# A graph layer on one core: another PSUM ring for one product, and a second engine for half of the copies in front of the router

## The chip, the core and the metric

The kernel runs on one core of a Trainium2 chip. The metric is the device time of one execution in microseconds. The profile comes from one further execution, and its times count from the start of its span. In the profile PE is TensorE (PEld its weight loads), DVE is VectorE, ACT is ScalarE, POOL is GpSimd and SP is SyncE, which issues most DMAs.

## What is computed

There are 1250 nodes of 1024 features and 40000 edges, sorted by target. A two-layer graph network is added to the input, and a mixture of experts is added to that:

```python
h   = relu(x_n @ W_self0 + mean0 @ W_neigh0 + b0)     # x_n = layernorm(x); mean over the sources of a node
out = h @ W_self1 + mean1 @ W_neigh1 + b1
x   = x + out
t   = layernorm(x)
logits = silu(t @ rw1 + rb1) @ rw2 + rb2              # router, top 2 of 8 experts
y   = t + sum_e w[t, e] * (silu(t @ ew1[e] + eb1[e]) @ ew2[e] + eb2[e])
out = x + y
```

All data is float32 in the reference.

## The kernel before, in words

The nodes are cut into ten blocks of up to 128 rows; the last one (block 9, `b9`) has 98. The work runs in stages, one after the other on PE: the counts of edges and the first layer (to 434 us), the second layer, the router (from about 778 us), and a loop over 23 tiles of tokens sorted by expert (from about 919 us).

**The second layer.** Its products by `W_neigh1` and `W_self1` go half by half of the columns, through `y_half` (twice) and `own_half` (twice, `h` = 0 and 1). Each of these four makes five pairs of blocks with `two_blocks` (lines 630 to 686): pairs 0 to 3 take the blocks j and 4+j, and the fifth pair takes the blocks 8 and 9. A pair is a Strassen-like scheme: seven products of four matmul steps each (line 648), in PSUM tiles `pa`, `pb` from the pool `mm` (tile name `ps`), and `pc`, `pd` from the pool `mmb` (tile name `psb`). Both pools have three buffers of one bank. In pairs 0 to 3 the product by `A22` is added to `pc` (line 679). In the fifth pair, where block 9 is shorter than 128 rows, it goes to a tile of its own, `pe` (line 682), taken from `mmb`, and `store` adds `u3` to it on DVE.

**What follows on each block.** In the last of the four halves, `own_half(w_last, ws_last, 1, finish)`, `finish(b)` runs for both blocks of a pair when its products are done (line 793). It calls `after_layers` (line 330): the layernorm (two `bn_stats` of 512 columns, lines 316 and 318, the aggregate, line 319, a square root on ACT, line 320, the reciprocal, line 322, and the 1024-wide normalisation on DVE, line 323), a store of the result to `t_d`, a POOL addition of the normalised row to `xa` (line 337), and a store of `xa` to the output (line 338). `finish` then hands the block to a queue of at most two, so that `turn_back` (line 805) works on the block that was finished two calls earlier. After the fifth pair `turn_back` empties the queue.

**`turn_back`.** A block is transposed on PE in two groups of four 128-column squares (line 814). A group is one tile of the pool `tpp` (`tp`, two buffers), of 4 x 128 float32 in each partition, which is one PSUM bank. Four copies of one square each bring it to `hT1`, where the router reads it; before the change ACT makes all four:

```python
for i in range(4):
    nc.scalar.copy(hT1[:, q + i, blk(b)], ps[:, i, :m])
```

**The router.** `moe` opens its own pools in the banks that `mm` and `mmb` leave. `route_two` is the same scheme as `two_blocks`, with 512-column operands: its sums of tokens (`token_sums`, T1, T2, T4) and T3 are written by DVE (line 140). T1, T2, T4 lie in `xw`, which takes the memory of `xa` and `more`, so T1 has to wait until the last block's store of `xa` has landed. `route(w0, 0, LAST)` (line 1167) is work on the last 226 tokens that PE does while T1 and T2 are made.

**What sets the order.** In these stages no order is written by hand. A planner walks the program in its order and puts the instructions on the engines' queues by its own model of their durations; at run time each engine takes its queue strictly in that order. It also sets the waits that the use of tiles needs. Orders written out by hand (`manual_schedule`) are in the opening and in the loop over tiles.

Of the kernel before, what the change touches and what calls it, by code (L numbers as in the profile page):

```python
# [10 lines left out]
F32 = mybir.dt.float32  # L11
# [10 lines left out]
P = 128  # L22
# [7 lines left out]
def kernel(  # L30
# [21 lines left out]
    nc = tc.nc  # L52
# [6 lines left out]
    QW = D // 4  # L59
# [14 lines left out]
    def blk(b):  # L74
        return slice(b * P, b * P + rows[b])
# [16 lines left out]
    hT1 = L[:, :NT].rearrange("p (k n) -> p k n", k=KD)  # L92
# [46 lines left out]
    def tt(o, a, b_, op):  # L139
        nc.vector.tensor_tensor(o, a, b_, op)  # L140
# [200 lines left out]
    def gnn_windows():  # L341
# [4 lines left out]
        mm = st.enter_context(tc.tile_pool(name="mm", bufs=3, space=PSUM))  # L346
# [177 lines left out]
        for q in range(4):  # L524
# [8 lines left out]
            if q == 0:  # L533
# [4 lines left out]
                for c0, n in cchunks:  # L538
                    ps = mm.tile([P, 512], F32, name="ps")
# [7 lines left out]
            for c0, n in cchunks:  # L547
                for d in (2 * q, 2 * q + 1):
                    ps = mm.tile([P, 512], F32, name="ps")
# [12 lines left out]
            if q == 0:  # L562

                dinv_p = small.tile([P, NB], F32, name="dinv_p")
                for b in range(NB):
                    m = rows[b]
# [7 lines left out]
        mmb = st.enter_context(tc.tile_pool(name="mmb", bufs=3, space=PSUM))  # L574
# [59 lines left out]
        def two_blocks(ws, j, u, store, amid=False):  # L634


            A11, A12, A22, S1, S2, S3, S4 = ws
            if j < NA:
                b, b2 = j, NA + j
                t1, t2, t3, t4 = (t[:, :, j * P : (j + 1) * P] for t in (T1, T2, T3, T4))  # L640
            else:
                b, b2 = b8, b9
                t1, t2, t3, t4 = Te1, Te2, Te3, Te4
            m2 = rows[b2]

            def product(ps, rows_of, w, first):
                for k in range(KB):
                    nc.tensor.matmul(  # L648
                        ps, rows_of(k), w[:, k, :], start=(first and k == 0),
                        stop=(k == KB - 1), skip_group_check=not first,  # L650
                    )

            u2, u3 = u[:, 0, :], u[:, 1, :]
            pa = mm.tile([P, 512], F32, name="ps")[:, :QW]
            product(pa, lambda k: hT1[:, k, blk(b)], A11, True)
            nc.scalar.copy(u2, pa)
            yield
            if amid:
                product(pa, lambda k: hT1[:, KB + k, blk(b)], A12, False)
                store(b, 0, pa, None)  # L660
                yield
            pb = mm.tile([P, 512], F32, name="ps")[:, :QW]
            product(pb, lambda k: t2[:, k, :], S2, True)
            tt(u2, u2, pb, ALU.add)
            if not amid:
                product(pa, lambda k: hT1[:, KB + k, blk(b)], A12, False)
                store(b, 0, pa, None)
            pc = mmb.tile([P, 512], F32, name="psb")[:, :QW]
            product(pc[:m2], lambda k: t3[:, k, :], S3, True)
            if m2 < P:  # L670

                past = slice(m2 // LQ * LQ, P)
                nc.scalar.copy(u3[past], u2[past])
            tt(u3[:m2], u2[:m2], pc[:m2], ALU.add)
            pd = mmb.tile([P, 512], F32, name="psb")[:m2, :QW]
            product(pd, lambda k: t1[:, k, :], S1, True)
            store(b2, 1, pd, u3[:m2])
            if m2 == P:
                product(pc, lambda k: t4[:, k, :], A22, False)
                store(b, 1, pc, u2)  # L680
            else:
                pe = mmb.tile([P, 512], F32, name="psb")[:, :QW]
                product(pe, lambda k: t4[:, k, :], A22, True)
                store(b, 1, pe, u3)
            product(pd, lambda k: hT1[:, KB + k, blk(b2)], S4, False)
            store(b2, 0, pd, u2[:m2])
# [16 lines left out]
        with tc.tile_pool(name="y1", bufs=1, side="right") as y1:  # L703
# [3 lines left out]
            def y_half(ws, h):  # L707
                def store(b, c, ps, u):
                    m = rows[b]
                    if u is not None:  # L710
                        t = spare()[:m]
                        tt(t, u, ps, ALU.add)
                        ps = t
                    cs = slice(c * QW, (c + 1) * QW)
                    split(yh[:m, b, cs], yl[:m, b, cs], ps)

                def pair(j, amid=False):
                    return two_blocks(
                        ws, j, us[:, 2 * (j % 2) : 2 * (j % 2) + 2, :], store, amid
                    )  # L720

                if h == 0:

                    two = [pair(j, True) for j in range(2)]
                    for _ in range(2):
                        for p in two:
                            next(p)
                    for p in two:
                        list(p)
                for j in range(0 if h else 2, NA + 1):  # L730
                    list(pair(j))
# [44 lines left out]
        def own_half(w, ws, h, done):  # L776
            def store(b, c, ps, u):
                m = rows[b]
                v = xa[:m, b, h * HALF + c * QW : h * HALF + (c + 1) * QW]
                if u is None:  # L780
                    tt(v, v, ps, ALU.add)
                else:
                    t = spare()[:m]
                    tt(t, u, ps, ALU.add)
                    nc.gpsimd.tensor_tensor(v, v, t, ALU.add)

            for j in range(NA + 1):
                list(two_blocks(ws, j, us[:, 2 * (j % 2) : 2 * (j % 2) + 2, :], store))
                if h == 0 and j == 1:
                    ws_last.extend(weight_sums(w_last, more[:, 2 * WQ : -2048]))  # L790
                for b in (j, NA + j) if j < NA else (b8, b9):
                    done(b)
# [3 lines left out]
        def finish(b):  # L796

            t = row_of((0, 1, 3)[n_done[0] % 3])
            n_done[0] += 1
            after_layers(b, xa, t)  # L800
            turned.append((b, t))
            if len(turned) > 2:
                turn_back()
# [3 lines left out]
        def turn_back():  # L807

            b, t = turned.pop(0)
            m = rows[b]  # L810
            for q in range(0, KD, 4):
                ps = tpp.tile([P, 4, P], F32, name="tp")
                for i in range(4):
                    nc.tensor.transpose(
                        ps[:, i, :m], t[:m, (q + i) * P : (q + i + 1) * P], ident[:m, :m]
                    )
                for i in range(4):
                    nc.scalar.copy(hT1[:, q + i, blk(b)], ps[:, i, :m])

        ws_last = []  # L820
        own_half(w_half, ws, 0, lambda b: None)
# [4 lines left out]
        while turned:  # L826
            turn_back()
# [920 lines left out]
```

## Time and profile before

| | us |
|---|---|
| median of 3 runs | 1121.33 |
| lowest, highest run | 1120.26, 1122.6 |
| the profiled execution | 1122.76 |
| its span in the profile | 1120.8 |
| PE busy | 1084.8 |
| DVE busy | 473.7 |
| ACT busy | 189.2 |
| POOL busy | 335.9 |

The profiled execution took 1122.76 us, 1.96 us more than its span, and 1.4 us more than the median. The copies of `turn_back` are 80 of 128 or 98 columns on ACT, between 735.1 and 785.1 us; the 72 wide ones had a mean of 285 ns. When several of them follow each other they overlap: 12 of them took 2.27 us from the start of the first to the end of the last.

In a line of the timeline the columns are the start in us, the duration in us, the engine, the line, the operation with output and input, and how many there are; in brackets stands the idle time before it and what ended it. In a line of the waits stand the waiting engine and the thing waited for, then the total in us, the number of times, and the longest. In the chain, each piece is the start, the length and the work.

### The profile page before, as it was taken

Reading aid. Unit: us, or ns where it says so; the run is one execution under the profiler, and the core shown is the slowest. Engines: PE = TensorE matmul, PEld = TensorE weight load, DVE = VectorE, ACT = ScalarE, POOL = GpSimd, SP = SyncE. Lnnn points to the kernel's source line nnn. Section 1 sums busy time; section 2 is a strip of 40 time slices with the busy share of each in tenths; the row PEclk is TensorE's granted clock in tenths of the full one; section 3 lists DMA queues with packets and bytes.
Section 4 is the critical chain, followed back from the end, with each engine's and each line's share of the span. In section 5 each row is a group of like instructions: output and inputs, shape, how many; then the busy total and the mean of one; then the engine's idle time right before and its main releaser. Section 6 shows DMA issues by size and latency. Waiting matters only on the chain.

```text
span 1120.8 us, 13458 instructions
## 1 busy us (share of the span) xinstructions
PE 1084.8 (97%) x4825; PEld 803.8 (72%) x4825; DVE 473.7 (42%) x1171; ACT 189.2 (17%) x431; POOL 335.9 (30%) x447
## 2 busy tenths in 40 slices
PE   6999999999999999999999999999999999999993
PEld 5555556888888888888888878887544487676762
DVE  8777787763121236332234132355522173222221
ACT  4301001001111111110011000023111134232321
POOL 2899999900000000013002202254000013332321
PEclk9999999999999999999999999999999999999997
DMA  7011011010100020033003280343970456767762
GB/s 241 30 38 39 2 38 39 1 38 1 38 1 1 1 75 20 1 113 120 27 1 142 101 275 1 94 174 152 321 228 1 150 188 169 193 178 193 194 170 47
DMA packets 62318, 107.34 MB, mean 96 GB/s; under 512 B 8906, under 2 KB 35690, under 8 KB 62240
## 3 DMA queue, kind: packets, MB, share of 16 engines
q1 hardware_dynamic: 51392, 79.69, 20.8%
q0 software_dynamic: 7056, 23.88, 9.1%
q10 hardware_dynamic: 3792, 2.79, 0.8%
q8 instruction: 42, 0.69, 0.3%
q14 instruction: 36, 0.29, 0.1%
HBM read 80.74 MB, written 27.42 MB: 96 GB/s over the span
## 4 chain that ended last, share of the span: by engine, by line
PE 75%; DMA 14%; DVE 4%; issue 4%; POOL 1%; ACT 1%; SPq 0%; POOLq 0%; DVEq 0%; ACTq 0%
PE ps L516 12%; DMA out_dram<-L 12%; PE ps L453 12%; PE psb L648 11%; PE ps L744 8%; PE ps L648 8%; PE ps L552 8%; PE ps L1214 4%; PE ps L1228 3%; PE cnt L414 3%; PE ps L1167 1%; DMA more<-in_L_gnn_W_self_dram 1%; DVE xw L140 1%; DVE L L140 1%; PE tp L306 1%
## 5 line engine op out<-in xcount | busy, mean ns | idle before, releaser
L404 POOL TENSOR_SCALAR ol<-lane,keys 125x128 f16<-125x128 f16 x320 | 193.8, 624 | 23.3 <-DVE oh L411 23.3
L453 PE MATMUL ps<-h0T,L 128*128 128x498 f32 (+2 forms) x384 | 148.0, 518 | 0.2 <-ACT h0T L309 0.2
L740 POOL TENSOR_TENSOR L<-L 128x512 f32<-128x512 f32 (+1 forms) x20 | 27.7, 1394 | 383.4 <-DMA L<-in_x_dram 383.4
L516 PE MATMUL ps<-L,h0T 128*128 128x256 f32 (+1 forms) x640 | 142.0, 379 | 0.0
L516 PEld LDWEIGHTS ps<-L,h0T 128*128 128x128 f32 (+1 forms) x640 | 118.4, 188 | 17.9 <-issue 0.5
L411 DVE TENSOR_SCALAR oh<-win,keys 125x240 f16<-125x240 f16 x320 | 82.9, 314 | 32.2 <-PE cnt L414 30.2
L453 PEld LDWEIGHTS ps<-h0T,L 128*128 128x128 f32 x384 | 67.6, 192 | 38.3 <-issue 34.0
L1559 PE MATMUL ps<-xw,L 128*128 x368 | 84.1, 380 | 0.7 <-issue 0.7
L1586 PE MATMUL ps<-xw,L 128*128 x184 | 82.8, 593 | 0.5 <-ACT L L1574 0.5
L552 PE MATMUL ps<-C,yh 128*128 128x256 f32 (+2 forms) x240 | 81.6, 355 | 0.0
L552 PE MATMUL ps<-C,yl 128*128 128x256 f32 (+2 forms) x240 | 81.3, 353 | 0.0
L744 PE MATMUL ps<-zh,C 128*128 128x512 f32 (+1 forms) x200 | 79.5, 397 | 0.0
L744 PE MATMUL ps<-zl,C 128*128 128x512 f32 (+1 forms) x200 | 78.6, 393 | 0.0
L1559 PEld LDWEIGHTS ps<-xw,L 128*128 128x128 f32 x368 | 68.0, 190 | 9.5 <-issue 1.4
L1592 POOL DMA_INDIRECT out_dram<-L x23 | 36.5, 1586 | 118.8 <-DVE L L1591 91.5
L433 DVE TENSOR_TENSOR C<-C,cnt 128x240 f32 x160 | 64.4, 403 | 12.9 <-DVE oh L411 1.4
L1531 POOL DMA_INDIRECT L<-t_d,L x26 | 25.5, 980 | 144.5 <-DVE L L140 123.7
L1586 PEld LDWEIGHTS ps<-xw,L 128*128 128x128 f32 x184 | 34.9, 190 | 34.9 <-issue 32.3
L414 PEld LDWEIGHTS <-ol 125*128 125x128 f16 x320 | 31.1, 97 | 37.7 <-POOL ol L404 19.8
L1591 DVE SCALAR_TENSOR_TENSOR L<-ps,L 128x512 f32<-128x512 f32 x46 | 34.5, 751 | 53.1 <-PE ps L1586 53.1
L648 PE MATMUL ps<-L 128*128 128x256 f32 x240 | 56.2, 379 | 0.0
L140 DVE TENSOR_TENSOR L<-L,ps 128x512 f32<-128x512 f32 (+1 forms) x30 | 18.0, 599 | 88.6 <-PE ps L1214 44.4
(232 smaller groups left out, 1512.2 us busy)
## 6 DMA issues: line engine op xcount, KB each, us to landing
xw<-in_L_ffn_ew_dram SPq DMA_DIRECT2D x16, 1024.0 KB, 9.9
L<-in_L_ffn_eb_dram SPq DMA_DIRECT2D x23, 512.0 KB, 4.1
L<-in_x_dram SPq DMA_DIRECT2D x20, 256.0 KB, 2.6
v_d<-L SPq DMA_DIRECT2D x18, 256.0 KB, 2.0
xa<-v_d SPq DMA_DIRECT2D x18, 256.0 KB, 7.8
t_d<-L SPq DMA_DIRECT2D x9, 512.0 KB, 3.0
out_dram<-xa SPq DMA_DIRECT2D x9, 512.0 KB, 2.6
L<-in_L_gnn_W_self_dram SPq DMA_DIRECT2D x4, 1024.0 KB, 8.2
```

Source lines behind the costliest of these rows:

```text
L404: nc.gpsimd.tensor_scalar(ol[:, c, :], lane[:GP], keys[:, 1, c, r : r + 1], None, op0=ALU.is_equal)
L411: nc.vector.tensor_scalar(oh, win[:GP], keys[:, 0, i * GC + c, r : r + 1], None, op0=ALU.is_equal)
L414: nc.tensor.matmul(ps[:, i, :GW], ol[:, i * GC + c, :], oh, start=(c == 0), stop=(c == GC - 1),)
L433: nc.vector.tensor_tensor(to, to.bitcast(F32), ps[:, i, :GW].rearrange("p (k w) -> p k w", k=NB), ALU.add,)
L453: nc.tensor.matmul(ps[:, :n], w[:, k, (d % 2) * P : (d % 2 + 1) * P], h0T[:, k, c0 : c0 + n], start=(k == 0), stop=(k == KD - 1),)
L516: nc.tensor.matmul(ps[:m, :QW], hT[:, k, blk(b)], w[:, k, :], start=(k == 0), stop=(k == KD - 1))
L552: nc.tensor.matmul(ps[:, :n], part[: rows[k], k, (d % 2) * P : (d % 2 + 1) * P], C[: rows[k], k, c0 : c0 + n], start=(k == 0 and part is y ...
L648: nc.tensor.matmul(ps, rows_of(k), w[:, k, :], start=(first and k == 0), stop=(k == KB - 1), skip_group_check=not first,)
L744: nc.tensor.matmul(ps[:m], C[: rows[k], k, blk(b)], part[: rows[k], k, :], start=(k == 0 and part is yh), stop=(k == NB - 1 and part is yl),)
L1214: nc.tensor.matmul(ps, a_[:, k, :], b_[:, k, :], start=(start and k == 0), stop=(stop and k == KB - 1),)
L1559: nc.tensor.matmul(ps[:, :H], xT[:, k, :], w1_all[:, ds(e, 1), k * H : (k + 1) * H], start=(k == 0), stop=(k == KD - 1),)
L1586: nc.tensor.matmul(ps, hT[:, q, :], w2_all[:, ds(e, 1), q * D + h * HALF : q * D + (h + 1) * HALF], start=(q == 0), stop=(q == KH - 1),)
```

## The change

`pe` of the fifth pair is taken from the pool `mm` (name `ps`) and no longer from `mmb`. Of the four copies of each group in `turn_back`, those with odd `i` run on DVE as `tensor_copy`, and those with even `i` stay on ACT. What is copied, and to where, is the same. No DMA, no matmul and no other instruction is added or removed.

```diff
@@ two_blocks
             else:
-                pe = mmb.tile([P, 512], F32, name="psb")[:, :QW]
+                pe = mm.tile([P, 512], F32, name="ps")[:, :QW]
                 product(pe, lambda k: t4[:, k, :], A22, True)
                 store(b, 1, pe, u3)
@@ turn_back
                 for i in range(4):
-                    nc.scalar.copy(hT1[:, q + i, blk(b)], ps[:, i, :m])
+                    copy = nc.vector.tensor_copy if i % 2 else nc.scalar.copy
+                    copy(hT1[:, q + i, blk(b)], ps[:, i, :m])
```

## The prediction, made before the result was known

> **What bounds the kernel now.** I read the page's busy times first, then PE's waits, then the timeline around the copies, and last the chain that ended last.
>
> ```profile
> PE 1084.8 (97%) x4825; PEld 803.8 (72%) x4825; DVE 473.7 (42%) x1171; ACT 189.2 (17%) x431; POOL 335.9 (30%) x447
> ```
>
> PE is busy for 97% of the span. From 434 us to the end of the router its records follow each other densely (eight matmul records of a second-layer product every 1.73 us), so what counts is where PE stands still. The waits of all engines between 730 and 802 us, the stretch that the copies lie in:
>
> ```profile
> DVE xw L140 <- DMA out_dram<-xa: 6.5, 1, 6.5
> ...
> PEld tp L814 <- ACT L L818: 3.6, 7, 1.0
> ...
> PE ps L1214 <- DVE L L140: 0.9, 1, 0.9
> ...
> PE tp L814 <- ACT L L818: 0.7, 3, 0.2
> ```
>
> PE waits for the copies three times, 0.7 us in all, and once for a DVE sum (0.9 us). The three waits are alike. This is PE in the first of the three bursts of transposes:
>
> ```profile
> 734.17 1.04 PE L814 MATMUL tp<-ident,L 128*128 128x128 f32 x8
> 735.05 0.60 PE L648 MATMUL ps<-more,L 128*128 128x256 f32 x2
> 735.88 0.66 PE L814 MATMUL tp<-ident,L 128*128 128x128 f32 x4 [0.24 <-ACT L L818]
> 736.37 0.60 PE L648 MATMUL ps<-more,L 128*128 128x256 f32 x2
> 736.81 0.60 PE L814 MATMUL tp<-ident,L 128*128 128x128 f32 x4
> 737.24 1.03 PE L648 MATMUL ps<-more,L 128*128 128x256 f32 x4
> 738.11 1.89 PE L648 MATMUL ps<-more,ts 128*128 128x256 f32 x8
> ```
>
> Eight transposes fill both `tp` buffers, then groups three and four wait until a buffer is empty, with parts of a product between them. Dense, sixteen transposes (0.88 us for eight, from 734.17 to 735.05, so 1.76) and eight product records (1.73) take 3.49 us; from 734.17 to 738.11 they took 3.94. So a burst loses 0.45 us, and the three bursts 1.35 us. That is all the copies cost PE before the fifth pair ends.
>
> The chain at the end of the second layer:
>
> ```profile
> 775.53 0.43 DVE more L140
> ...
> 776.79 0.70 DVE st L318
> ...
> 779.28 0.69 DVE st L318
> ...
> 780.83 1.60 DVE L L323
> ...
> 782.56 2.36 POOL xa L337
> ...
> 784.94 3.71 DMA out_dram<-xa
> ...
> 788.94 2.35 DVE xw L140 x2
> 791.75 6.29 DVE xw L140 x5
> 798.04 2.21 DVE L L140
> ...
> 800.30 4.99 PE ps L1214 x11
> ```
>
> Here PE is not the bound. From 775.53 us DVE ends the fifth pair and does the layernorms of blocks 8 and 9, POOL adds, a DMA lands at 788.65, and only then may DVE write T1 and the sums after it. PE fills the time with router work on other columns, runs out of it, and waits 0.9 us at 800.30. Whatever delays DVE in front of the last normalisation (780.83 to 782.43) delays 800.30 by as much: there is no slack between them, and PE is dense after it.
>
> **The change part by part.**
>
> **The PSUM place.** Four products (one for each half) change their pool. No matmul is added. In the fifth pair `mm` then holds `pa`, `pb`, `pe` in its three buffers and `mmb` only `pc`, `pd`. Before, PE goes through the end of every half without a wait (the waits of PE between 434 and 648 us are empty, and those from 648 to 710 us are two of 0.6 us, where DVE, held by sums of weights, reads late what PE adds to next). The next taker of an `mm` buffer after `pe` finds `pa`'s empty: in the last fifth pair the DVE addition that frees `pa` starts at 770.35, five microseconds before `pe` is done. In the router the new pool lies where `mm` lay; `pe` is freed by the DVE addition that starts at 775.53 (0.42 us), and the first router matmul comes at 778.26, held by a copy. The cover is 2.3 us. I cost it at 0; if the cover were gone, at most these 2.3 us once, and as a gain also 0, since no wait of PE there is for an empty buffer of `mmb`.
>
> **The copies' price.** 40 of 80 copies leave ACT and come to DVE. ACT does them at 0.18 us each (12 in 2.27). No DVE copy of 128 columns out of PSUM is in the trace. Near rows: a DVE reduction of 128x128 from a `tp` tile, 292 ns (L1277); a DVE copy of 128x256 from PSUM, 425 ns (L1565). From the slope of the clock of these two (133 ns for 128 columns) a 128-column copy is about 290 ns long. Back to back, DVE rows of this size start some 60 ns sooner than their length (two of 1024 columns, 2.36 us, instead of two times 1.22). So 0.23 us is the lower bound of a copy's time on DVE, 0.29 the value where something has to wait for its end. The Trainium skill (Perfetto Trace Analysis, Optimizing Scalar/DVE Operations) gives a fixed share of about 125 ns for DVE on PSUM and 51 ns for ScalarE: an estimate of 0.26 us against 0.16, which lies in my bracket and says too that the copy moves to the dearer engine.
>
> **Side by side, or in turn?** By the sum so far a group would empty in about 0.55 us (two engines, two copies each) against 0.75 before (four in the rows of ACT at 738.33). Against that stands the Trainium skill, PSUM — Partial Sum Buffer, PSUM bank collisions raise a hardware error: two engines may not touch the same bank of the same partitions at once, two readers included, and software has to keep them apart. A group is exactly one bank. No row of before has ACT and DVE reading one bank without one needing the other's result, so the trace can't show whether the planner puts waits between them. Without waits: 0.55 us for a group. With waits the four copies run in turn, ACT, DVE, ACT, DVE: 0.285 + 0.29 + 0.285 + 0.29 and three hand-overs of 0.03 (the aggregate on DVE ends at 777.73, the root on ACT starts at 777.76) make 1.24 us. I take the second, since the colliding read would be an error. Two groups may then overlap, so the rate need not suffer; the latency of a buffer does, by 0.5 us, and each copy on DVE now also waits for ACT, and the ACT copy behind it for DVE.
>
> **The three bursts (734, 748, 763 us).** DVE is in its densest stretch there, from 733.90 to about 740.3: four `bn_stats`, two normalisations of 1.25 and 1.31 us and two additions. Eight copies come in, 8 x 0.23 = 1.8 us at least. Behind them stand the second block's layernorm and the additions of the next pair; these have cover (a buffer of `mmb` is needed again only a product group later, the next transposes of these blocks come with the next pair), so they cost nothing. On the path is only the `tp` buffer. The third group of transposes started at 735.88 and would start 0.5 us later; the fourth may find its copy behind a normalisation, up to 1.25 us later. PE's product records between them hide part, if the planner has put enough of them there: eight of them, 1.73 us, are all there is of this product. Bounds for a burst: -0.45 (all loss gone) and +1.3. The trace has DVE busy for nearly all of the burst, so I stay on the upper side of the middle: +0.45 each, +1.35 us in all.
>
> **The tail (777 to 786 us).** Here 16 copies come to DVE. Program order puts the copies of block 3 between the layernorms of blocks 8 and 9, and those of block 7 behind the latter. Four copies on the chain at 0.23 are 0.9 us; with hand-overs each can hold DVE for up to an ACT copy more (0.29 + 0.285 + 0.03 = 0.6), 2.4 us. If DVE idle time takes them (0.36 us at 780.21 while the root is made), the least is 0.5. If block 7's copies get ahead too, another 0.9. I take 1.5 us. ACT gains what DVE loses (16 x 0.18 = 2.9 us), but PE's gain from that ends at the wait at 800.30. T1, T2 and T3 move with the landing of block 9's store. Queues: no DMA is moved; POOL's two additions and SP's two stores wait for DVE as before, later by the same 1.5.
>
> Sum: 0 + 1.35 + 1.5 = 2.85 us. The profiled execution would have a span of 1123.65 and a time of 1125.6. The median lies 1.4 us below the profiled time, so 1121.33 + 2.85, rounded to 1124.1 us.
>
> **The rivals.**
>
> Nearly nothing changes. Planner and hardware tuck the DVE copies into gaps, the bursts cost what they cost, and the tail pays about 0.9 us for four copies: some 1122.0. For it: DVE is busy in only 7 to 11 of each 15 us there. Against it: the gaps aren't where the copies become ready.
>
> Faster. The two engines empty a bank side by side in 0.55 us, the three PE losses go (1.35 us), and the tail's DVE chain comes earlier with them: 1119.9, at the utmost 1118.5 with the tail's own PE loss (the dense sum of 777.06 to 785.73 is 7.7 of 8.67 us, 0.9). It decides at one point: whether the DVE copy of groups one and two starts before the 1.25 us normalisation at 736.00. If it does, the buffer is back before 735.8.
>
> Much slower. The planner, with other durations in its sum, orders PE's and DVE's queues anew, and copies stand behind normalisations in every burst: three times 1.3 and a tail of 2.4, 6.3 us, 1127.6; half of that in the bursts, 1125.7. I write it at 1126.5.
>
> That the change doesn't do what it says is in my main case: in turn, and not side by side.
>
> **How the numbers follow.** A difference of 0.2%, 2.2 us, is about what a measurement of this kernel can tell from no change. Main case, chance 0.52, own range 1122.3 to 1125.8; of it 0.37 is over 1123.6 and 0.15 below. Much slower, 0.20, all over. Nearly nothing, 0.16, within. Faster, 0.12: 0.08 beyond 0.2%, 0.04 within. So faster 0.08, same 0.35, slower 0.57. The range 1119.8 to 1127.5 leaves out half of the faster case and the end of the slower one, under 0.2.
>
> **What would show it.** Groups of L818 would appear with about forty rows on DVE and forty on ACT, and in the timeline the four copies of a group in turn with no overlap between the engines; overlapping rows would refute that step. PE's waits at L814 would name DVE, over 0.7 us in all. The start of the last L323 (780.83) and the first router sum (788.94), measured from the end of the fifth pair (775.53), would come 0.5 to 2.4 us later. The wait at L1214 for DVE would grow from 0.9. No wait of PE would name the buffers of `pe`. I am wrong if the bursts become dense, if the distance from 775.53 to 800.30 doesn't grow, or if the difference sits outside 730 to 802 us.

## The result, and the profile after

The changed kernel took 1122.99 us (median of 12 runs, 1122.43 to 1123.91), the kernel before 1121.3 us (median of 12, 1119.85 to 1122.6). The ratio is 1.0016, with a 95% interval of 1.0009 to 1.0024: slower by 1.0 to 2.7 us. The prediction was 1124.1 us, 2.85 over before; about 1.8 came (the two medians lie 1.69 apart). In the two traces the distance from the first burst of transposes to the first product by T3 grew by 1.43 us. Of this 1.34 lies in the three bursts, where the prediction had put 1.35, and next to nothing in the tail behind them, where it had put 1.5.

The busy times on the page of the changed kernel:

```profile
PE 1085.2 (97%) x4825; PEld 803.6 (72%) x4825; DVE 479.0 (43%) x1211; ACT 184.8 (16%) x391; POOL 335.7 (30%) x447
```

Forty instructions moved from ACT to DVE (1211 for 1171, 391 for 431); PE's work is what it was. The waits between 730 and 803 us (waiting engine, what it waited for, then total, times, longest):

```profile
ACT L L819 <- DVE L L819: 10.8, 12, 1.3
...
PE tp L814 <- DVE L L819: 1.7, 3, 0.6
...
PE ps L1215 <- DVE xw L140: 0.8, 1, 0.8
```

The three waits of PE in front of transposes are still three, but now 0.56 us each for DVE, where they were 0.24 for ACT. The first row is new in kind: a ScalarE copy waits for a VectorE copy, twelve times. The first burst shows why (timeline of the changed kernel; start, duration, engine, work, and in brackets the idle time before it):

```profile
734.03 1.04 PE L814 MATMUL tp<-ident,L 128*128 128x128 f32 x8
...
734.90 1.89 PE L648 MATMUL ps<-more,L 128*128 128x256 f32 x8
734.94 0.43 ACT L819 COPY L<-tp 128x128 f32<-128x128 f32 x2
...
735.74 0.27 DVE L819 COPY L<-tp 128x128 f32<-128x128 f32 x1
...
735.93 1.18 DVE L323 TENSOR_SCALAR L<-xa,mv,rs 128x1024 f32<-128x1024 f32 x1
736.04 0.27 ACT L819 COPY L<-tp 128x128 f32<-128x128 f32 x1 [0.67 <-DVE L L819]
737.02 0.47 DVE L819 COPY L<-tp 128x128 f32<-128x128 f32 x2
...
737.36 0.65 PE L814 MATMUL tp<-ident,L 128*128 128x128 f32 x4 [0.56 <-DVE L L819]
```

Read it by bank. ACT makes the first copy of both groups (734.94). DVE makes the second of group one at 735.74; ACT's third starts at 736.04, 0.03 us after DVE's ended at 736.01. The fourth would be DVE's, but the normalisation (735.93 to 737.11) stands before it in DVE's queue, so it comes at 737.02. The third group of transposes starts behind it at 737.36, 3.33 us after the start of the burst; before, it was 1.71 us after it. PE had eight product records in front of it, not two, and still waited.

The chain at the end of the second layer, changed kernel (start, length, work):

```profile
776.73 0.43 DVE more L140
...
786.14 3.48 DMA out_dram<-xa
...
789.91 2.29 DVE xw L140
792.20 0.17 DVE L L819
792.37 5.61 DVE xw L140 x4
```

From the store of the fifth pair's own product (775.53 before, 776.73 here) to the first token sum (788.94 and 789.91) the distance is 13.41 us before and 13.18 here: this part of the tail did not grow. New is a copy of block 9 at 792.20, inside the sums. Two more rows of the changed kernel, POOL's last addition and the first product by T3:

```profile
783.75 2.36 POOL L337 TENSOR_TENSOR xa<-xa,L 98x1024 f32<-98x1024 f32 x1 [0.70 <-DVE L L323]
...
801.59 3.60 PE L1215 MATMUL ps<-L,xw 128*128 128x512 f32 x8
```

PE does not wait in front of this product any more; its 0.8 us for DVE (the third row of the waits) now stands in front of an earlier one, at 798.08.

### The profile page after: what moved, and what is told of

It reads as the page before. It is cut to its first block, busy times and chain, and to the rows that moved or that the text cites. A ratio compares the mean times of both kernels' runs of the same rounds, so it can differ in the third digit from the quotient of the medians.

```text
span 1121.6 us, 13448 instructions
## 1 busy us (share of the span) xinstructions
PE 1085.2 (97%) x4825; PEld 803.6 (72%) x4825; DVE 479.0 (43%) x1211; ACT 184.8 (16%) x391; POOL 335.7 (30%) x447
## 4 chain that ended last, share of the span: by engine, by line
PE 75%; DMA 15%; issue 4%; DVE 3%; POOL 1%; ACT 1%; SPq 0%; POOLq 0%; ACTq 0%; DVEq 0%
DMA out_dram<-L 12%; PE ps L516 12%; PE ps L453 12%; PE psb L648 10%; PE ps L648 8%; PE ps L744 8%; PE ps L552 8%; PE ps L1215 5%; PE ps L1229 3%; PE cnt L414 3%; PE ps L1168 2%; DMA more<-in_L_gnn_W_self_dram 1%; PE tp L306 1%; DVE xw L140 1%; POOL ol L404 1%
## 5 line engine op out<-in xcount | busy, mean ns | idle before, releaser
L648 PE MATMUL ps<-L 128*128 128x256 f32 x264 | 61.9, 379 | 0.0
```

Source lines behind the costliest of these rows:

```text
L648: nc.tensor.matmul(ps, rows_of(k), w[:, k, :], start=(first and k == 0), stop=(k == KB - 1), skip_group_check=not first,)
```

## The experiments

All times stand against runs of the kernel before on the same chip: first the two medians, then the ratio with its 95% interval, which is not the quotient of the medians. A second measure comes from each trace. I call it the **stretch**: from the first transposes behind the second pair to the DVE store of the fifth pair's own product. The same PE work lies in it in every kernel, and the three bursts: 41.36 us before (734.17 to 775.53), 42.70 after (734.03 to 776.73). It comes from one trace of each kernel; within each of these two traces the three bursts agree to 0.01 us. In the two kernels where transposes are spread, it starts at the product that takes their place at that point.

### The place alone

```diff
-                pe = mmb.tile([P, 512], F32, name="psb")[:, :QW]
+                pe = mm.tile([P, 512], F32, name="ps")[:, :QW]
```

> Only the PSUM place of the fifth pair's own product is changed, the copies stay on ScalarE. If the place costs nothing (my step), the time is that of before within 0.7 us and each burst of transposes keeps its 0.45 us of loss. If the place carries part of the change, this run is slower by up to the 1.7 us that the change cost.

1121.71 us against 1121.73, ratio 1.0000 (0.9992 to 1.0009); stretch 41.36. The place costs nothing.

### The copies alone

```diff
-                    nc.scalar.copy(hT1[:, q + i, blk(b)], ps[:, i, :m])
+                    copy = nc.vector.tensor_copy if i % 2 else nc.scalar.copy
+                    copy(hT1[:, q + i, blk(b)], ps[:, i, :m])
```

> Only the copies are split between ScalarE and VectorE, the place stays. If the copies carry all of it, about 1.7 us over before, three waits of about 0.56 us at the third group of transposes, and a loss of 0.9 us in each burst. If the place carries part, less than that.

1123.15 against 1121.73, ratio 1.0013 (1.0004 to 1.0022); three waits of 0.56 us; stretch 42.69. The copies carry the whole change.

### A group to one engine, all copies on VectorE, two and two

Three kernels change which engine takes which of the four copies of a group; the rest is the changed kernel.

```diff
-                    copy = nc.vector.tensor_copy if i % 2 else nc.scalar.copy
+                    copy = nc.vector.tensor_copy if q else nc.scalar.copy        # a group to one engine
+                    copy = nc.vector.tensor_copy                                 # all on VectorE
+                    copy = nc.vector.tensor_copy if i > 1 else nc.scalar.copy    # two and two
```

> As the changed kernel, but all four copies of a group go to one engine: the first group of a block to ScalarE, the second to VectorE. The same 40 copies are on VectorE, and no bank is read by two engines. If the turns within a bank cost the time, the wait at the third group falls to 0.25 us or less and the time comes back to before or below it (1120.5 to 1121.5). If VectorE's load costs it (copies queued behind normalisations), the waits stay at about 0.5 us and the time stays 1.5 us above before.

1121.85 against 1121.73, ratio 1.0001 (0.9993 to 1.0010); stretch 42.02. VectorE makes as many copies as in the changed kernel, and half of the loss in the bursts is gone (0.66 us over before, not 1.34); the wait at the third group is back at 0.24. What is left shows at the fourth group, which here waits for ScalarE copies too (0.40 us at its weight load).

> As the changed kernel, but all 80 copies are on VectorE: no bank is read by two engines, and VectorE's added load is doubled. If the load costs the time, twice the loss of the change or more: 3 us or more above before. If the turns cost it, less than the change costs: under 1.5 us above before.

1122.23 against 1121.73, ratio 1.0001 (0.9992 to 1.0010); stretch 42.24. Twice the copies on VectorE cost less in the stretch (0.88 us) than half of them in turns. The load theory, in which the loss grows with the number of VectorE copies, falls as the whole cause. A part of it stands: with no bank shared, 40 copies on VectorE lengthen the stretch by 0.66 us and 80 by 0.88.

> As the changed kernel, but the first two copies of a group go to ScalarE and the last two to VectorE, so that a bank changes hands once and not three times. If the turns within a bank set the loss, a burst takes between 7.39 us (before) and 7.84 us (changed), near 7.6, and the kernel about 0.7 us over before. If not the number of hand-overs but VectorE's place in the group sets it, it stays at 7.84.

1123.03 against 1121.82, ratio 1.0008 (0.9995 to 1.0021), not to be told from before by its time; stretch 42.53. The bank changes hands once, and the loss is 1.17 us, nearly that of three times. So the number of hand-overs does not set it. Its first burst:

```profile
734.29 0.75 ACT L819 COPY L<-tp 128x128 f32<-128x128 f32 x4
735.09 0.27 DVE L819 COPY L<-tp 128x128 f32<-128x128 f32 x1
735.28 1.18 DVE L323 TENSOR_SCALAR L<-xa,mv,rs 128x1024 f32<-128x1024 f32 x1
...
736.38 0.67 DVE L819 COPY L<-tp 128x128 f32<-128x128 f32 x3
...
736.80 1.07 PE L814 MATMUL tp<-ident,L 128*128 128x128 f32 x8 [0.65 <-DVE L L819]
```

ACT is done with both banks at 735.04. One VectorE copy slips in ahead of the normalisation, three stand behind it, and PE waits for these, 0.65 us.

### One copy for the whole group

```diff
-                for i in range(4):
-                    copy = nc.vector.tensor_copy if i % 2 else nc.scalar.copy
-                    copy(hT1[:, q + i, blk(b)], ps[:, i, :m])
+                nc.scalar.copy(hT1[:, q : q + 4, blk(b)], ps[:, :, :m])
```

> As the changed kernel, but the four copies of a group are one copy of 512 columns on ScalarE. Before, four took 0.75 us; one of 512 columns takes 0.59 us elsewhere in the trace. If the time in which a bank empties sets the loss, a burst takes 0.1 to 0.3 us less than before (7.1 to 7.3), and the kernel is at before or up to 0.9 us under it. If the first copies of a group let other work start, which one copy would hold back, it is above before.

1122.77 against 1121.82, ratio 1.0007 (0.9997 to 1.0017); stretch 42.06, 0.70 us longer than before. A miss: a bank empties sooner (two copies in 1.05 us, 0.59 each alone), and the bursts get longer. The third group starts 1.53 us after the start of the burst (732.77 to 734.30), and not 1.71. But the planner now puts it right behind the second, with no product record between, and PE waits 0.49 us there. What matters is not how fast a bank empties, but how that compares with the place of the next group in PE's queue.

### A third bank

```diff
-        mmb = st.enter_context(tc.tile_pool(name="mmb", bufs=3, space=PSUM))
+        mmb = st.enter_context(tc.tile_pool(name="mmb", bufs=2, space=PSUM))
+        tpx = st.enter_context(tc.tile_pool(name="tpx", bufs=1, space=PSUM))
...
-                ps = tpp.tile([P, 4, P], F32, name="tp")
+                ps = (tpx if n_turn[0] % 3 == 2 else tpp).tile([P, 4, P], F32, name="tp")
+                n_turn[0] += 1
```

With the split copies:

> The changed kernel with its split copies, but a third bank for turned rows: the second ring of the second layer keeps two buffers, which is possible since the fifth pair's own product lies in the first ring, and the freed bank takes every third group. If the loss is the time that a bank takes to empty, the third group finds an empty bank, a burst comes down to 7.2 us or less and the kernel to 2 us under the changed one. If VectorE's load or the planner's order costs it, the third bank changes nothing: 7.84 us. A rival cost: with two buffers in the second ring TensorE may wait for them between pairs.

1122.65 against 1121.82, ratio 1.0011 (1.0001 to 1.0021); stretch 42.32. With all copies on ScalarE (the fifth pair's product lies in `mm` here too):

> The third bank, but all copies on ScalarE as before. If the time to empty a bank is the loss, the bursts are near dense (6.95 to 7.1 us) and the kernel is 1 to 1.3 us under before. If two buffers in the second ring cost waits, those take it back.

1121.32 against 1121.82, ratio 0.9995 (0.9986 to 1.0005); stretch 41.35. Misses again: neither kernel became as fast as expected. With a third bank twelve transposes go through at once, then the fourth group waits, 0.56 us with split copies and 0.23 with ScalarE alone, as the third had done. A bank more only moves the place where PE meets a full one. Two buffers in the second ring were enough: no wait of PE between 730 and 803 us names them.

### Groups spread over the next pair

```diff
             def product(ps, rows_of, w, first):
...
+                if groups_due:
+                    groups_due.pop(0)()
...
-            t = row_of((0, 1, 3)[n_done[0] % 3])
+            t = (row_of(0), row_of(1), row_of(3), S_first[:, :D])[n_done[0] % 4]
...
-            for q in range(0, KD, 4):
+            def turn_group(q):
...
+            groups_due.extend(partial(turn_group, q) for q in range(0, KD, 4))
...
+        for group in groups_due:
+            group()
```

With all copies on ScalarE:

> All copies on ScalarE as before, but the groups of transposes of a block are no longer asked for together behind a pair: each comes behind one product of the next pair, and a fourth row holds the normalised blocks meanwhile. If the loss in a burst comes from groups that stand in TensorE's queue before a bank is empty, there are no waits at the transposes up to the end of the fifth pair, and the kernel is about 1.35 us under before (1120.0 to 1120.8). If the transposes cost more than their own time in another way, it stays at before.

1120.42 against 1121.86, ratio 0.9983 (0.9973 to 0.9993), the fastest kernel of the study; stretch 40.00 us, 1.36 shorter than before. PE around the place of the first burst:

```profile
734.08 0.60 PE L819 MATMUL tp<-ident,L 128*128 128x128 f32 x4
734.52 1.89 PE L650 MATMUL ps<-more,ts 128*128 128x256 f32 x8
736.25 0.60 PE L819 MATMUL tp<-ident,L 128*128 128x128 f32 x4
736.68 1.89 PE L650 MATMUL ps<-more,L 128*128 128x256 f32 x8
738.41 0.60 PE L819 MATMUL tp<-ident,L 128*128 128x128 f32 x4
```

A group and a product take 2.17 us each time, no bracket stands behind any, and a bank has two products' time to empty. The fourth row came with this change; since no wait of PE in the stretch before names a row, the gain is put down to the new places. With the split copies of the changed kernel:

> The changed kernel with the same spreading. If the turns of two engines in one bank only cost by making a bank late for the next group, they cost nothing here: no waits at the transposes up to the end of the fifth pair, and the time within 0.7 us of the spread kernel with ScalarE alone. If VectorE's copies cost by their load, this kernel stays 1 to 1.7 us above that one.

1121.61 against 1121.86, ratio 0.9995 (0.9986 to 1.0004); stretch 40.37. In the first two pairs the copies in turn cost nothing; the third holds the remaining 0.37, of it one wait of 0.2 us at the transposes. But this kernel was 1.2 us slower than the one with ScalarE alone, where up to 0.7 was expected. That lies in the range of the rival, VectorE's load (1 to 1.7); the intervals of the two ratios overlap, though. The trace shows part of it behind the stretch: PE waits for VectorE copies at two router products (0.8 and 0.5 us), and the first token sum comes only at 787.60 though the last store had landed by 786.66, with a small sum and two copies of block 9 ahead of it.

### GpSimd's addition left out

In both kernels, for block 8 alone, so that its output lacks that term. Each ran once (1121.74 and 1121.69 us), so only the traces are read:

```diff
-        nc.gpsimd.tensor_tensor(xa[:m, b, :], xa[:m, b, :], t[:m], ALU.add)
+        if b != 8:
+            nc.gpsimd.tensor_tensor(xa[:m, b, :], xa[:m, b, :], t[:m], ALU.add)
```

> The kernel before, without GpSimd's addition of the normalised row for block 8, so that block's output lacks that term. If GpSimd's addition stretches the normalisation of block 9 that runs beside it (1.59 us), that one takes 0.8 to 1.0 us here, and from the store of the fifth pair's own product to its end it is 0.6 to 0.8 us shorter than 6.89 us. If not, both stay.

> The changed kernel, also without GpSimd's addition for block 8. If the stretch hid the copies that stand on VectorE ahead of block 9's normalisation, its end comes here later than in the kernel before without that addition, by 0.4 to 0.7 us. If the copies cost nothing there for another reason, both ends lie at the same distance.

First the two kernels as they are; the kernel before (POOL's addition for block 8, then the normalisation of block 9):

```profile
779.51 2.36 POOL L337 TENSOR_TENSOR xa<-xa,L 128x1024 f32<-128x1024 f32 x1 [0.69 <-DVE L L323]
...
780.83 1.59 DVE L323 TENSOR_SCALAR L<-xa,mv,rs 98x1024 f32<-98x1024 f32 x1
```

and the changed kernel:

```profile
780.70 2.35 POOL L337 TENSOR_TENSOR xa<-xa,L 128x1024 f32<-128x1024 f32 x1 [0.69 <-DVE L L323]
...
782.62 0.98 DVE L323 TENSOR_SCALAR L<-xa,mv,rs 98x1024 f32<-98x1024 f32 x1
```

The normalisation starts 5.30 us after the fifth pair's store before, and 5.89 after: the copies do push it, by 0.59. But it ends 0.55 us after POOL's addition in both (782.42 and 781.87; 783.60 and 783.05). Without the addition, the kernel before:

```profile
775.62 0.42 DVE L140 TENSOR_TENSOR more<-more,psb 128x256 f32<-128x256 f32 x1 [1.30 <-PE psb L649]
...
780.92 0.81 DVE L323 TENSOR_SCALAR L<-xa,mv,rs 98x1024 f32<-98x1024 f32 x1
```

and the changed kernel:

```profile
775.45 0.42 DVE L140 TENSOR_TENSOR more<-more,ps 128x256 f32<-128x256 f32 x1 [1.31 <-PE ps L649]
...
781.35 0.81 DVE L323 TENSOR_SCALAR L<-xa,mv,rs 98x1024 f32<-98x1024 f32 x1
```

Both take 0.81 us. From the store to the end of the normalisation it is 6.11 us in the first and 6.71 in the second; with the addition 6.89 and 6.87. So the copies cost 0.60 us here once the stretched normalisation is gone, and 0.0 beside it. Shown, by one trace of each.

## Why the prediction was right, and where not

**The PSUM place, 0 us.** Right: 1.0000 alone, the same stretch to 0.01 us, and no wait for an `mm` buffer.

**A copy's price.** The length was right (0.278 us median against 0.29). My lower bound was too high: where eight follow each other (the kernel with a group to one engine) they take 1.66 us, from start to start (1.66 - 0.28) / 7 = 0.20 us, and not 0.23. A slip is part of it: the two rows that I used start 2.36 - 1.22 = 1.14 us apart, 80 ns under their length and not 60, which makes 0.21. The estimate of 0.26 us taken from the Trainium skill (Perfetto Trace Analysis, Optimizing Scalar/DVE Operations) lies above the measured distance from start to start and below the measured length; the measured figures hold.

**In turn, not side by side.** Right. The order ACT, DVE, ACT within one bank, with 0.03 us between DVE and ACT (736.01 to 736.04), is in the first burst above; between two different banks the engines do overlap (four ScalarE and four VectorE copies of one block in 1.65 us, from 783.27 to 784.92). In the first burst, as far as the rows tell the banks apart, no two copies of one bank overlap. The bank rule that the prediction cited from the Trainium skill (PSUM — Partial Sum Buffer, PSUM bank collisions raise a hardware error) is in line with this; whether the chip needs these waits no run here shows.

**The three bursts, +1.35 us.** Right in size and place: each takes 7.84 us to the next pair's first `psb` product, 7.39 before, three times 0.45. That it agrees to 0.01 us is luck: I had picked the value between bounds of -0.45 and +1.3, and not worked it out. The reason was right in one half. The normalisation in front of the last copy was named; the half microsecond for hand-overs was a minor part, since one hand-over costs nearly as much as three (1.17 of 1.34 us). And I had the loss as a bank that is late. The runs show it as a difference: a group waits when the planned order has too little other work in front of it for the time that the bank takes. In the first burst PE had product work left behind the waiting group. A faster emptying (one copy) and a third bank did not help, other places in the queue did.

**The tail, +1.5 us.** This step failed. It said that whatever delays DVE in front of the last normalisation delays the router as much. It put 1.5 us on the distance from the fifth pair's store to the first product by T3, and said that I am wrong if that distance doesn't grow. It went from 24.77 us (775.53 to 800.30) to 24.86 (776.73 to 801.59): 0.09. The start of the last normalisation did come 0.59 later; its end did not, and from the store to the end of POOL's last addition it is 9.38 us in both kernels (775.53 to 784.91, 776.73 to 786.11). The copies took 0.6 us there, at the low end of my range, and a normalisation that is slow beside POOL and fast behind it gave all of it back, as the two runs without the addition show, by one trace of each. I had read its 1.59 us as its own duration, though the same line stood at 1.08 us for the block before. What the tail did cost lies later: the block 9 copy among the token sums and another order of these, from the first sum to the first product by T3 11.36 us before and 11.68 after (789.91 to 801.59), 0.32 us. The kernel with the copies alone has the 11.68 too, the one with a group to one engine 11.36. The last store and what stands between it and the first sum gave back 0.23.

**The sum.** 1.34 in the bursts and 0.09 in the tail make the 1.43 of the two traces. The last store in it (3.71 us before, 3.48 after, 2.93 with the place alone) varies too much from run to run to carry a part; with equal stores it is 1.34 + 0.32 = 1.66. Both lie inside the measured 1.0 to 2.7. So 2.85 was too much by the tail, and the main case held in its lower part, below 1123.6 us, to which I had given 0.15 and not the 0.37 above. (1121.33 + 2.85 is 1124.18, so the rounded value should have been 1124.2.) The rivals: "nearly nothing" was nearer in the tail, with 0.9 us, but had no place for the bursts. "Faster" failed at the point it named, since the first bank's last VectorE copy came behind the normalisation. Of "much slower", the new order did come, and cost only what the bursts show.

What stays open: why the kernel with split copies spread over the next pair is 1.2 us above the one with ScalarE alone. Up to the first product by T3 the two traces differ by 1.34 us from the start of the stretch: 0.37 in the stretch and 0.97 behind it, 0.69 of that in the last store (2.95 and 3.64 us). Two waits and late copies are seen too, but no run took them away one by one.

## What to carry to other kernels

Where engines take queues in a planned order, price a slower release by the work that stands in front of the next taker in its queue, not by the buffer alone: asking for the transposes one group at a time, each behind a product, gained the 1.36 us that neither a third bank nor a faster copy could. Work split over two engines that must take turns is as late as the later queue; look at what is the longest instruction ahead of it there (here 1.18 us, against 0.28 for the copy). And before charging a delay in full on a chain, ask whether the next instruction on it is stretched by a neighbour, and would be faster if it came later.

## What the runs showed of the hardware

A VectorE normalisation of 98 rows of 1024 columns took 0.81 us alone, and 1.59 where GpSimd added rows beside it. Twelve traces have both that normalisation (block 9) and GpSimd's addition for block 8. In ten of them it starts 0.3 to 1.1 us before the addition ends, and it ends 0.54 to 0.55 us behind it, wherever it had started. In the kernel with two and two copies it starts only 0.14 us before GpSimd's end (782.11 against 782.25) and takes its 0.81; with all copies on VectorE it starts later still and takes 0.80. So it behaves as if it made about a quarter of a microsecond of way (an estimate: 0.81 less 0.55) and then stood until GpSimd had finished.

The normalisation that the copies wait behind in the first burst is of this kind too: it ends at 737.11, 0.56 us behind a GpSimd addition of line 785 (735.83 to 736.55). So a part of its 1.18 us, and of the copies' lateness, would be GpSimd's; no run left that addition out.

The Trainium skill tells of such a lock (SBUF — State Buffer, Who interferes with whom: a VectorE instruction in a two-port mode and GpSimd exclude each other for a whole instruction). A normalisation that stands until GpSimd has finished agrees with it, and the two runs without the addition take the stretch away; whether it ran in such a mode no run shows.
